# A running count over 0/1 tiles: the lower half of an old tile and the upper half of a new one in one matmul

## The chip, the cores and the metric

The kernel runs on one core of a Trainium2 chip. The engines that matter here are TensorE (PE, matrix products into PSUM), VectorE (DVE), ScalarE (ACT) and GpSimd (POOL); SyncE (SP) issues the loads. Each engine works through its own queue in order and waits on semaphores for the others. The metric is the device time of one launch in microseconds (us).

## The reference, cut to what matters

Four graph layers run over one dense adjacency matrix of 3327 x 3327, mostly zeros, with 64 features a node. Layers 0 and 1 are a gated update and a hyperbolic layer, layer 3 is attention over pairs of nodes. The change is in layer 2, which weights each neighbour by how many neighbours come after it in the row:

```python
support = input @ weight
mask = (adj != 0).astype(support.dtype)
rank = jnp.cumsum(mask, axis=1)
deg = rank[:, -1:]
k = jnp.minimum(deg, float(MAX_NEIGH))        # MAX_NEIGH = 100
pos = rank - (deg - k)
w = mask * jnp.where(pos > 0, DECAY ** (k - pos), 0.0)   # DECAY = 0.5
out = w @ support + bias
```

So an entry of a row counts 0.5 to the power of the number of nonzero entries to its right (as far as 100 of them). The kernel walks over the columns from the last to the first and keeps a running count in PSUM.

## The kernel before, in words

The 3327 nodes are padded to 26 blocks of 128. The adjacency lies turned in memory: a tile has 128 source nodes on the partitions and a group of target nodes along the free axis. There are two groups of targets, group 1 (two halves of 896, 1792 in all) and group 0 (two halves of 768, 1536 in all); a half is called h, and `g.w` is its width. Each half is worked in two chunks for the matmuls (384 and 512, or 384 and 384), called q.

**Layer 2** goes over 52 tiles, first the 26 of group 1, then those of group 0, from the last sources to the first. Tiles come in pairs: n even (a=1) and n odd (a=0), m is the even one. The steps of a tile are:

- `mask(n)` (L1833, DVE): the f32 adjacency tile becomes a bf16 0/1 tile. Five mask buffers are used in turn, so mask n+5 waits until the last count that reads mask n is done. A mask also frees the adjacency slot from which SP's next load goes on.
- `count(n, h)` (matmuls at L1864): adds to a running count in PSUM (`cnt[h]`, one pair of banks for each h). Each matmul has 64 output columns; s = 0 and 1 fill the lower and the upper 64 partitions of the output, and the two stand side by side on the array. For a=0 the terms are `tri_a` on masks m and m+1. For a=1 there are two terms: `rest_a` on the two masks of the pair before (m-2, m-1), and `tri_b` on masks m and m+1. `rest_a` has nonzero weights only for the mask's partitions 0 to 63, `tri_b` only for partitions 64 to 127; the other halves are zeros. So a step from one half block to the next takes out the diagonal of the old half and adds that of the new one.
- after the count, the weights `w` (L1876, ACT; four of the 104 on DVE, L1874, where the list says so): the running count as bits of a bf16 exponent, which is the power of 0.5. The next count for the same h waits for this reading of PSUM.
- `weigh(n, q)` (L1886, PE): the weights times the support, in three bf16 parts, into the layer's accumulators. Per n and q that is six matmuls.

**What sets the order.** For layers 2 and 3 all steps stand in one list, `ORDER3`; the program goes through it and each step appends its instructions to the queues of its engines. Steps with one letter are pieces of chains that run between: u and v finish layer 1 and make layer 2's input for the two groups, n makes layer 3's node data for group 1 (with xw transfers issued from POOL, L1175 and L1176), s the same for group 0, b, f and e are the ends. After `l3` the buffers of layer 3 are opened and cleared on POOL (memsets of `pack`, L1946, and `p2c`, L1947). The last steps of layer 2 are mixed with the first of layer 3 (tanh_t, tanh_d, distances, gelus, attention, square).

**Loads.** The adjacency tiles (896 or 768 KB) come through SP's queue into a pool of slots; the order of use is read off the same list (mask and attention steps).

**Constants.** `tri_b`, `tri_a`, `rest_a` and `ones64` are made once near the start by DVE. `rest_a[D:]`, which is all zeros, also serves layer 3 as the zero weights of `cleared`, which zeroes PSUM banks.

Of the kernel before, what the change touches and what calls it, by code (L numbers as in the profile page):

```python
# [9 lines left out]
BF16 = mybir.dt.bfloat16  # L10
# [8 lines left out]
D = 64  # L19
P = 128  # L20
# [54 lines left out]
GROUPS = [Group(0, 6), Group(6, HB)]  # L75
# [149 lines left out]
def order3(text):  # L225
# [14 lines left out]
    count.0.0 count.0.1 u u u count.1.0 count.1.1 mask.2 mask.3 mask.4 u count.2.0 count.2.1  # L240
    v count.3.0 count.3.1 u weigh.0.0 weigh.0.1 weigh.1.0 v mask.5 count.4.0 count.4.1
    weigh.1.1 count.5.0 count.5.1 mask.6 mask.7 mask.8 weigh.2.0 weigh.3.0 v v weigh.2.1
    weigh.3.1 weigh.4.0 weigh.5.0 count.6.0 count.6.1 weigh.4.1 count.7.0 weigh.5.1
    count.7.1 mask.9 count.8.0 mask.10 count.8.1 mask.11 weigh.6.0 count.9.0 v weigh.7.0
    count.9.1 weigh.8.0 count.10.0 count.10.1 mask.12 mask.13 weigh.6.1 count.11.0 weigh.9.0
    count.11.1 weigh.10.0 count.12.0 count.12.1 v v v mask.14 weigh.11.0 mask.15 weigh.7.1
    count.13.0 count.13.1 weigh.8.1 weigh.9.1 v v weigh.10.1 count.14.0 count.14.1 mask.16
    mask.17 weigh.12.0 weigh.11.1 weigh.13.0 count.15.0 count.15.1 v v count.16.0 count.16.1
    mask.18 mask.19 v count.17.0 count.17.1 weigh.12.1 weigh.13.1 v count.18.0 count.18.1
    mask.20 mask.21 mask.22 weigh.14.0 weigh.14.1 count.19.0 count.19.1 weigh.15.0  # L250
    weigh.16.0 weigh.17.0 count.20.0 count.20.1 mask.23 weigh.15.1 weigh.16.1 count.21.0
    count.21.1 weigh.17.1 weigh.18.0 weigh.19.0 count.22.0 count.22.1 mask.24 mask.25
    weigh.18.1 weigh.19.1 count.23.0 weigh.20.0 weigh.20.1 count.23.1 weigh.21.0 count.24.0
    count.24.1 mask.26 mask.27 mask.28 weigh.22.0 weigh.21.1 count.25.0 count.25.1 mask.29
    weigh.23.0 weigh.22.1 weigh.23.1 count.26.0 count.26.1 weigh.24.0 weigh.25.0 count.27.0
    count.27.1 weigh.24.1 weigh.25.1 l3 mask.30 count.28.0 count.28.1 mask.31 n n n
    weigh.26.0 weigh.26.1 count.29.0 count.29.1 n n weigh.27.0 weigh.28.0 weigh.27.1
    count.30.0 count.30.1 weigh.28.1 count.31.0 count.31.1 weigh.29.0 weigh.29.1 mask.32
    mask.33 n count.32.0 mask.34 count.32.1 mask.35 mask.36 weigh.30.0 weigh.30.1 count.33.0
    count.33.1 n n n weigh.31.0 weigh.32.0 weigh.31.1 count.34.0 count.34.1 weigh.32.1  # L260
    weigh.33.0 weigh.33.1 count.35.0 mask.37 mask.38 weigh.34.0 weigh.34.1 count.35.1 n n
    count.36.0 count.36.1 mask.39 weigh.35.0 n n n n count.37.0 count.37.1 mask.40
    weigh.36.0 weigh.35.1 count.38.0 count.38.1 weigh.36.1 weigh.37.0 n n count.39.0
    count.39.1 weigh.38.0 weigh.37.1 mask.41 count.40.0 n n mask.42 count.40.1 mask.43
    mask.44 weigh.38.1 count.41.0 weigh.39.0 weigh.40.0 count.41.1 n n n n weigh.39.1
    count.42.0 count.42.1 n n n n weigh.40.1 count.43.0 count.43.1 weigh.41.0 weigh.41.1
    mask.45 count.44.0 count.44.1 mask.46 weigh.42.0 weigh.43.0 weigh.42.1 count.45.0
    count.45.1 mask.47 n n n n weigh.43.1 n mask.48 count.46.0 count.46.1 mask.49 weigh.44.0
    weigh.44.1 count.47.0 n n tanh_t.0.0.0 tanh_t.0.1.0 n count.47.1.1 weigh.45.0 weigh.45.1
    count.48.0 count.48.1 weigh.46.0 weigh.47.0 mask.50 mask.51 weigh.46.1 count.49.0  # L270
    count.49.1.1 n weigh.47.1 tanh_t.0.1.1 tanh_t.0.0.1 count.50.0 count.50.1.1 tanh_d.0.0
    weigh.48.0 weigh.48.1 count.51.0 count.51.1.1 distances.0.0.0 distances.0.0.1
    gelus.0.0.0 gelus.0.0.1 distances.0.1.0 attention_t.0.0 distances.0.1.1 weigh.49.0
    weigh.49.1 gelus.0.1.0 gelus.0.1.1 weigh.50.0 weigh.51.0 attention_d.0.0 weigh.50.1
    square.0.0 weigh.51.1 wk tanh_d.1.1 evict distances.1.0.0 gelus.1.0.0 attention_t.0.1
    tanh_d.0.1 factors_d.0.0 s distances.1.0.1 gelus.1.0.1 tanh_t.1.0.0 tanh_t.1.1.0 s
    clear.0 square.0.1 s gather_d.0.0 s s distances.1.1.0 turned.0.0.0 factors_t.0.0.0
    turned.0.0.1 factors_t.0.0.1 turned.0.1.0 clear.1 gelus.1.1.0 s distances.1.1.1
    factors_t.0.1.0 s clear.2 singles.0.0 gelus.1.1.1 turned.0.1.1 tanh_d.1.0
    attention_d.0.1 distances.2.0.0 gelus.2.0.0 gather_t.0.0.0 s square.1.0 factors_t.0.1.1  # L280
    s gather_t.0.1.1 s gather_t.0.0.1 s square.1.1 factors_d.0.1 attention_t.1.0
    attention_d.1.0 gather_t.0.1.0 attention_t.1.1 distances.2.0.1 gelus.2.0.1 factors_d.1.0
    s gather_d.0.1 s turned.1.0.0 tanh_t.2.0.0 tanh_t.2.0.1 distances.2.1.0 s s s s s
    gelus.2.1.0 distances.2.1.1 tanh_d.2.0 gelus.2.1.1 square.2.0 factors_t.1.0.0
    gather_d.1.0 attention_d.1.1 attention_t.2.0 turned.1.1.0 distances.3.0.0 gelus.3.0.0
    singles.1.0 square.2.1 singles.0.1 tanh_t.2.1.0 distances.3.0.1 factors_t.1.1.0
    turned.2.0.0 factors_d.1.1 factors_t.2.0.0 s s gelus.3.0.1 distances.3.1.0 tanh_t.2.1.1
    s s gelus.3.1.0 turned.2.0.1 s distances.3.1.1 gelus.3.1.1 attention_d.2.0
    factors_t.2.0.1 s s turned.2.1.0 tanh_d.2.1 distances.4.0.0 factors_d.2.0 gelus.4.0.0 s
    s s gather_d.2.0 square.3.1 attention_t.2.1 attention_d.2.1 gather_t.1.1.0  # L290
    gather_t.1.0.0 gather_t.2.0.1 gather_t.2.0.0 factors_t.2.1.0 gather_t.2.1.0
    factors_d.2.1 s turned.2.1.1 tanh_t.3.0.0 distances.4.0.1 square.3.0 factors_t.2.1.1
    turned.3.0.0 singles.2.0 singles.1.1 tanh_t.3.0.1 attention_t.3.0 factors_t.3.0.0
    tanh_d.3.0 attention_d.3.0 s s gelus.4.0.1 turned.3.0.1 factors_t.3.0.1 factors_d.3.0
    tanh_t.3.1.0 tanh_t.3.1.1 distances.4.1.0 s gelus.4.1.0 gather_d.1.1 tanh_d.3.1
    turned.3.1.0 attention_t.3.1 factors_t.3.1.0 distances.4.1.1 gelus.4.1.1 s s
    gather_t.2.1.1 square.4.0 gather_d.3.0 gather_t.3.0.0 attention_d.3.1 factors_d.3.1
    gather_d.2.1 turned.3.1.1 distances.5.0.0 tanh_t.4.0.0 tanh_t.4.0.1 factors_t.3.1.1 s
    singles.2.1 square.4.1 turned.4.0.0 attention_t.4.0 factors_t.4.0.0 gelus.5.0.0
    distances.5.0.1 gather_t.3.1.1 gather_d.3.1 tanh_d.4.0 attention_d.4.0 turned.4.0.1  # L300
    gelus.5.0.1 distances.5.1.0 factors_d.4.0 tanh_d.4.1 tanh_t.4.1.0 tanh_t.4.1.1
    singles.3.1 singles.3.0 factors_t.4.0.1 attention_t.4.1 s b turned.4.1.0 factors_t.4.1.0
    gelus.5.1.0 distances.5.1.1 b tanh_d.5.0 gather_t.3.1.0 attention_d.4.1 factors_d.4.1
    gather_t.3.0.1 turned.4.1.1 factors_t.4.1.1 gelus.5.1.1 distances.6.0.0 tanh_t.5.0.0
    tanh_t.5.0.1 attention_t.5.0 attention_d.5.0 square.5.0 singles.4.0 z gather_t.4.1.0
    gather_d.4.1 square.5.1 gather_t.4.0.0 turned.5.0.0 factors_t.5.0.0 gelus.6.0.0
    distances.6.0.1 tanh_t.5.1.0 tanh_t.5.1.1 attention_t.5.1 gather_d.4.0 turned.5.0.1
    factors_t.5.0.1 gelus.6.0.1 distances.6.1.0 tanh_d.5.1 attention_d.5.1 gather_t.4.0.1
    gather_t.4.1.1 gather_t.5.0.0 square.6.0 turned.5.1.0 gelus.6.1.0 distances.6.1.1
    singles.4.1 factors_d.5.0 singles.5.0 factors_t.5.1.0 turned.5.1.1 tanh_t.6.0.0  # L310
    tanh_t.6.0.1 attention_t.6.0 factors_t.5.1.1 gelus.6.1.1 distances.7.0.0 tanh_t.6.1.0
    factors_d.5.1 gather_t.5.1.0 square.6.1 turned.6.0.0 factors_t.6.0.0 gelus.7.0.0
    distances.7.0.1 tanh_d.6.0 attention_d.6.0 gather_d.5.0 gather_t.5.0.1 tanh_t.7.0.0
    factors_d.6.0 gather_t.6.0.0 turned.6.0.1 factors_t.6.0.1 gelus.7.0.1 tanh_t.6.1.1
    distances.7.1.0 singles.5.1 attention_t.6.1 turned.6.1.0 factors_t.6.1.0 tanh_d.6.1
    gelus.7.1.0 square.7.0 distances.7.1.1 gather_d.5.1 attention_d.6.1 turned.6.1.1
    factors_t.6.1.1 gelus.7.1.1 distances.8.0.0 tanh_t.7.0.1 attention_t.7.0 singles.6.0
    square.7.1 turned.7.0.0 factors_t.7.0.0 gelus.8.0.0 distances.8.0.1 gather_t.6.1.1
# [2052 lines left out]
```

## Time and profile before

| what | value |
|---|---|
| median of 3 runs | 647.39 us (647.32 to 648.18) |
| the profiled execution | 643.85 us, span 642.0 us |
| granted PE clock, mean | 0.989 |
| loads and stores | 183.40 MB, mean 286 GB/s |
| layer 2, first count to last weigh | 279.4 to 411.6 us of the span |
| count matmuls (L1864) | 208 with tri_b, 208 with tri_a, 192 with rest_a, 8 with ones |
| weigh matmuls (L1886) | 624 |
| weights on ACT (L1876) | 100, mean 953 ns |
| masks on DVE (L1833) | 52, of which 50 in the stretch of layer 2 |
| POOL busy in the whole span | 25.3 us |

Busy times of an engine count the time of its instructions. For PE they count each matmul from its start to its modelled end, so that matmuls which follow one another closely overlap in the records; how dense PE's work is, is better read from the distance between starts. POOL's spans are rough. A row of a group shows line, engine, operation, output and input names and shapes, count, then busy us, mean ns of one, and the idle time before them with what ended it. A row of the timeline shows start, duration, engine, line and operation.

### The profile page before, as it was taken

To read this page: it belongs to the slowest core of one execution; us is meant where nothing else is said; L and a number is where in the kernel's file an instruction comes from. 1 tells how busy PE (TensorE), PEld (TensorE's weight loads), DVE (VectorE), ACT (ScalarE), POOL (GpSimd) and SP (SyncE) were. 2 spreads that over 40 slices of the span, in tenths; PEclk is the share of its full clock that TensorE was granted. 3 is DMA by queue.
4 is the path that set the end of the run, shared out by engine and by line. 5 is a ranking of instruction groups with operands and counts; after the bars stand their busy time and mean duration, and the time that the engine had idled before them with its cause. 6 is when DMAs were issued, how large, how long until landed. Compare 5 with 4: busy or idle time off the path is not lost.

```text
span 642.0 us, 13208 instructions
## 1 busy us (share of the span) xinstructions
PE 601.1 (94%) x5592; PEld 321.8 (50%) x5592; DVE 450.2 (70%) x687; ACT 378.4 (59%) x528; POOL 25.3 (4%) x48
## 2 busy tenths in 40 slices
PE   2987999899998999999999999989999999999992
PEld 1442444334332433346777776546655555556660
DVE  3230876454488760567864866999999999999955
ACT  3110400130254420369987979999999998999734
POOL 0000000000000000030000010017000000000000
PEclk9999999999999999999999999989999999999996
DMA  8999999449998799999978895519676776755401
GB/s 334 415 417 418 364 393 339 177 157 392 418 417 368 282 415 419 417 365 400 359 277 292 300 329 225 189 58 288 206 246 211 251 235 226 240 177 196 153 2 59
DMA packets 32531, 183.40 MB, mean 286 GB/s; under 512 B 3696, under 2 KB 4752, under 8 KB 32464
## 3 DMA queue, kind: packets, MB, share of 16 engines
q1 hardware_dynamic: 32112, 181.63, 75.4%
q0 software_dynamic: 352, 0.85, 0.5%
q8 instruction: 45, 0.74, 0.5%
q14 instruction: 22, 0.18, 0.1%
HBM read 180.76 MB, written 0.85 MB: 283 GB/s over the span
## 4 chain that ended last, share of the span: by engine, by line
PE 78%; DMA 8%; DVE 6%; ACT 5%; issue 1%; SPq 0%; DVEq 0%; ACTq 0%
PE bank L772 25%; PE bank L1493 18%; PE pair L1368 8%; DMA adj<-in_adj 8%; PE bank L1886 7%; PE pair L1864 7%; PE pair L1483 4%; PE pair L873 3%; ACT w L1876 2%; PE pair L677 1%; DMA xn<-in_x 1%; PE bank L647 1%; PE bank L1755 1%; ACT tr L1438 0%; DVE mask L1833 0%
## 5 line engine op out<-in xcount | busy, mean ns | idle before, releaser
L772 PE MATMUL bank<-adj,m_a 128*64 128x384 f32 (+1 forms) x832 | 153.5, 516 | 8.9 <-DMA adj<-in_adj 6.5
L772 PEld LDWEIGHTS bank<-adj,m_a 128*64 128x64 f32 x832 | 57.1, 137 | 95.0 <-issue 71.3
L1876 ACT ACTIVATE w<-pair,ebias 128x896 uint16<-128x896 f32 (+1 forms) x100 | 90.1, 953 | 14.6 <-PE pair L1864 14.4
L772 PE MATMUL bank<-adj,m_b 128*64 128x384 f32 (+1 forms) x416 | 76.7, 515 | 1.4 <-ACT hm L861 1.4
L499 DVE SCALAR_TENSOR_TENSOR edges<-adj,edges 128x1792 bf16<-128x1792 f32 (+1 forms) x24 | 45.0, 1890 | 31.3 <-DMA adj<-in_adj 31.2
L1833 DVE TENSOR_SCALAR mask<-adj 128x1792 bf16<-128x1792 f32 (+1 forms) x52 | 51.7, 1025 | 18.4 <-PE pair L1864 18.2
L861 ACT ACTIVATE hm<-bank 64x384 f32<-64x384 f32 (+1 forms) x8 | 4.1, 512 | 94.5 <-DVE mh L860 94.2
L1886 PE MATMUL bank<-w,m_b 128*64 128x384 bf16 (+1 forms) x416 | 55.9, 340 | 0.1
L772 PEld LDWEIGHTS bank<-adj,m_b 128*64 128x64 f32 x416 | 28.8, 137 | 45.8 <-issue 41.5
L1368 PE MATMUL pair<-xs 64*128 64x384 f32 (+3 forms) x120 | 50.8, 507 | 0.5 <-ACT s L1384 0.5
L1368 PE MATMUL pair<-xs,xw 64*128 64x384 f32 (+3 forms) x120 | 50.8, 507 | 0.0
L1409 ACT ACTIVATE d<-leftb,righth 128x768 f32<-128x768 f32 (+3 forms) x45 | 38.7, 918 | 0.1
L1886 PE MATMUL bank<-w,h_t 128*64 128x384 bf16 (+1 forms) x208 | 38.2, 339 | 0.1
L1449 DVE SCALAR_TENSOR_TENSOR d<-d,adj 128x1792 f32<-128x1792 f32 x19 | 38.3, 2014 | 0.0
L1864 PE MATMUL pair<-mask,tri_b 128*64 128x384 bf16 (+1 forms) x208 | 37.0, 339 | 0.0
L1864 PE MATMUL pair<-mask,rest_a 128*64 128x384 bf16 x192 | 33.5, 341 | 0.1
L1493 PE MATMUL bank<-d,xd 128*64 128x384 f32 (+3 forms) x236 | 32.2, 411 | 0.5 <-ACT sq L1625 0.5
L1886 PEld LDWEIGHTS <-m_b 128*64 128x64 bf16 x416 | 27.3, 110 | 10.6 <-issue 1.5
L1490 DVE SCALAR_TENSOR_TENSOR tr<-pair,tr 128x1024 f32<-128x1024 f32 (+3 forms) x28 | 26.7, 954 | 4.0 <-PE pair L1483 3.5
L1438 ACT ACTIVATE tr<-leftb,righth 128x512 f32<-128x512 f32 (+1 forms) x48 | 28.7, 660 | 0.4 <-PE bank L1493 0.4
L1493 PE MATMUL bank<-d,p2c 128*32 128x128 f32 (+1 forms) x348 | 28.5, 322 | 0.0
L1864 PE MATMUL pair<-mask,tri_a 128*64 128x384 bf16 x208 | 25.8, 341 | 0.7 <-ACT w L1876 0.7
(371 smaller groups left out, 1089.0 us busy)
## 6 DMA issues: line engine op xcount, KB each, us to landing
adj<-in_adj SPq DMA_DIRECT2D x108, 896.0 KB, 6.5
adj<-in_adj SPq DMA_DIRECT2D x94, 768.0 KB, 8.7
adj<-in_adj SPq DMA_DIRECT2D x8, 640.0 KB, 5.1
adj<-in_adj SPq DMA_DIRECT2D x2, 512.0 KB, 3.9
xn<-in_x SPq DMA_DIRECT2D x3, 192.0 KB, 4.8
out<-s SPq DMA_DIRECT2D x3, 192.0 KB, 2.6
xw<-xs POOLq DMA_DIRECT2D x4, 128.0 KB, 4.9
w_l<-in_w_l SPq DMA_DIRECT2D x1, 460.0 KB, 9.9
```

Source lines behind the costliest of these rows:

```text
L499: V.scalar_tensor_tensor(e, a, 0.0, e, op0=OP.not_equal, op1=OP.add)
L772: T.matmul(acc[q][h * D : (h + 1) * D, : hi - lo], lhsT=m[:, k, :], rhs=a[:, h * g.w + lo : h * g.w + hi], start=first, stop=last,)
L1368: T.matmul(p[k][:, o : o + n], lhsT=l, rhs=r, start=not rows, stop=rows)
L1409: S.activation(columns(dirs[m, b], ph.n)[:, :, first * P : first * P + n], left_of(ph.g)[:, :, o : o + n], AF.Tanh, bias=righth[:, 2 * c + ...
L1438: S.activation(by_rows(a, m, u)[:, x : x + 2 * n].rearrange("p (b e) r c -> p b e r c", b=2), left_of(ph.s)[:, :, o : o + n * P].rearrange ...
L1449: V.scalar_tensor_tensor(a[:, :w], a[:, :w], 1.0, stream.tile(stream.now), op0=OP.add, op1=OP.mult)
L1490: V.scalar_tensor_tensor(a, p, rest_of(m), a, op0=OP.add, op1=OP.mult)
L1493: T.matmul(out, lhsT=lhsT, rhs=rhs, start=False, stop=True, skip_group_check=True)
L1833: V.tensor_scalar(masks[n][:, :w], a, 0.0, None, op0=OP.not_equal)
L1864: T.matmul(cnt[h][s * D : (s + 1) * D, P + lo : P + hi], lhsT=l, rhs=r, start=first and j == 0, stop=j == len(terms) - 1 or first and s == ...
L1876: S.activation(w, e, AF.Relu, bias=ebias)
L1886: T.matmul(acc2[i][q][h * D : (h + 1) * D, : hi - lo], lhsT=p[:, 2 * c + a, :], rhs=ws[n][:, h * g.w + lo : h * g.w + hi].bitcast(BF16), s ...
```

## The change

Before the count of an even tile pair (a=1, all but the first pair of a group), a new step `pre(n, h)` copies partitions 64 to 127 of masks m and m+1 over partitions 64 to 127 of masks m-2 and m-1, for the half h. Those old tiles then hold the old pair's lower 64 sources and the new pair's upper 64. `tri_b` holds `rest`'s weights in its lower half and `tri`'s in its upper half, so one term with `tri_b` on the old tiles does what two terms did. The copies for h=0 are issued on DVE, those for h=1 on POOL: 24 pairs x 2 halves x 2 tiles = 96 copies of 64 partitions x `g.w` bf16. `rest_a` is gone (with its memset and copy, and `tri_b`'s memset); the first pair of a group uses only the upper half of `tri_b` and of the masks; `cleared` takes its zeros from a block of the identity off the diagonal.

```diff
-    tri_b, tri_a, rest_a, ones64 = (
-        p0.tile([P, D], BF16, name=n) for n in ("tri_b", "tri_a", "rest_a", "ones64")
-    )
+    tri_b, tri_a, ones64 = (p0.tile([P, D], BF16, name=n) for n in ("tri_b", "tri_a", "ones64"))
...
-        V.memset(tri_b, 0.0)
+        V.tensor_copy(tri_b[:D], rest[:D, :D])
         V.tensor_copy(tri_b[D:], tri[D:, D:])
         V.tensor_copy(tri_a[:D], tri[:D, :D])
         V.tensor_copy(tri_a[D:], rest[D:, D:])
-        V.memset(rest_a, 0.0)
-        V.tensor_copy(rest_a[:D], rest[:D, :D])
...
-                    lhsT=rest_a[D:],
+                    lhsT=identb[D:, :D],
...
+        def pre(n, h):
+
+            g = GROUPS[work[n][0]]
+            m = n - n % 2
+            cs = slice(h * g.w, (h + 1) * g.w)
+            for s in range(2):
+                E = (V, G)[((0, 3)[h] >> s) & 1]
+                E.tensor_copy(masks[m - 2 + s][D:, cs], masks[m + s][D:, cs])
+
...
                 if first:
-                    terms.append([(ones64, edges[i][:, cs]), (tri_b, masks[m + 1][:, cs])])
-                    terms.append([(tri_b, masks[m][:, cs])])
+                    terms.append([(ones64, edges[i][:, cs]), (tri_b[D:], masks[m + 1][D:, cs])])
+                    terms.append([(tri_b[D:], masks[m][D:, cs])])
                 elif a:
-                    terms.append([(rest_a, masks[m - 2 + s][:, cs]) for s in range(2)])
-                    terms.append([(tri_b, masks[m + s][:, cs]) for s in range(2)])
+                    terms.append([(tri_b, masks[m - 2 + s][:, cs]) for s in range(2)])
                 else:
...
-        STEPS3.update(mask=mask, count=count, weigh=weigh)
+        STEPS3.update(mask=mask, count=count, weigh=weigh, pre=pre)
```

The list `ORDER3` is written anew from its first step on: it has the 48 `pre` steps, and the other steps stand in another order. A stretch of it, before and after:

```diff
-    count.31.1 weigh.29.0 weigh.29.1 mask.32
-    mask.33 n count.32.0 mask.34 count.32.1 mask.35 mask.36 weigh.30.0 weigh.30.1 count.33.0
-    count.33.1
...
+    count.31.1 mask.32
+    mask.33 pre.32.0 weigh.29.0 weigh.30.0 weigh.29.1 count.32.0 pre.32.1 count.32.1
+    weigh.30.1 n count.33.0 mask.34 mask.35 pre.34.0 count.33.1 pre.34.1
```

The number of masks, counts, weigh steps and loads is the same in both; the four weight passes on DVE are the same ones (tiles 47, 49, 50 and 51, h=1). Two steps that stood before the last weigh, gelus.0.1.1 and square.0.0, stand after it now. Layers 0 and 1 are not touched.

## Prediction

> **What bounds the kernel now.** I read the page's busy shares and chain of waits first, then the windows of layer 2, then its groups by engine, and last the POOL and DVE timelines, because the change puts POOL to work beside DVE.
>
> ```profile
> PE 601.1 (94%) x5592; PEld 321.8 (50%) x5592; DVE 450.2 (70%) x687; ACT 378.4 (59%) x528; POOL 25.3 (4%) x48
> PE 78%; DMA 8%; DVE 6%; ACT 5%; issue 1%; SPq 0%; DVEq 0%; ACTq 0%
> 279.40:411.60 132.20, 131.07 (x1455) 93.17 (x1455) 94.43 (x152) 114.65 (x145) 5.35 (x9) 1.00 0.83 302
> 430.00:610.00 180.00, 179.79 (x2300) 105.33 (x2302) 174.60 (x125) 169.05 (x208) 13.75 (x27) 1.00 0.66 218
> ```
>
> The windows give start:end, length, then busy us of PE, weight loads, DVE, ACT and POOL, the granted clock, the DMA share and GB/s. From the first count to the last weigh layer 2 takes 132.2 us: PE is full, ACT busy 114.7, DVE 94.4. Layer 3 after it has DVE at 97% and PE and ACT near it.
>
> "Busy" counts a matmul's latency, so I recount PE by starts. In the timeline a pair of 64-column matmuls (upper and lower output half, side by side) starts 0.163 us after the one before at 384 columns and 0.213 us at 512. The stage has 930 narrow and 310 wide bf16 ones: 465 x 0.163 + 155 x 0.213 = 108.8. Its other PE groups add about 19.7 (their busy times, pairs counted once). That is 128.5 of 132.2, or 97%: PE bounds layer 2, and 97% is what this kind of listing reaches on its tightest resource.
>
> ```profile
> L1864 PE MATMUL pair<-mask,rest_a 128*64 128x384 bf16 x144 | 24.4, 328 | 0.1
> L1864 PE MATMUL pair<-mask,rest_a 128*64 128x512 bf16 x48 | 9.7, 379 | 0.0
> L1876 ACT ACTIVATE w<-pair,ebias 128x896 uint16<-128x896 f32 (+1 forms) x100 | 90.1, 953 | 14.6 <-PE pair L1864 14.4
> L1833 DVE TENSOR_SCALAR mask<-adj 128x1536 bf16<-128x1536 f32 (+1 forms) x50 | 49.6, 1023 | 18.4 <-PE pair L1864 18.2
> ```
>
> ACT waits 14.4 us for counts and DVE's masks wait 18.2 us for counts to free their buffers: a shorter count helps both, as long as nothing new stands in front of it.
>
> **What it removes.** All 192 rest_a matmuls: 72 x 0.163 + 24 x 0.213 = 16.8 us of PE. The tri_b matmuls that stay have 128 rows in use instead of 64; their duration doesn't depend on it (tri_a uses all 128 rows already, 328 against tri_b's 326 ns). PE keeps 128.5 - 16.8 = 111.7. ACT keeps its 104 weight passes less the four on DVE; one gelus (0.92, L1384) and one square (2.0, L1390) slip behind the last weigh: ACT 113.7, DVE 92.4. The memset and copy of constants lie in the load-bound start: nothing, and 1 us if that cover went.
>
> **What it adds.** 24 tile pairs get `pre`: two copies of 64 x 896 (12 pairs) or 64 x 768 on DVE for h=0, and two on POOL for h=1. No row has this copy. On DVE the nearest is the cast out of and into on-chip memory:
>
> ```profile
> L1077 DVE CAST m_b<-sq 128x896 bf16<-128x896 f32 x1 | 0.6, 629 | 0.0
> L1946 POOL MEMSET pack<- 128x1792 bf16 x2 | 3.1, 1592 | 274.9 <-DMA adj<-in_adj 274.9
> L1947 POOL MEMSET p2c<- 128x988 f32 x1 | 1.8, 1805 | 6.2 <-DVE mask L1833 6.2
> 283.65 3.08 DVE L1833 TENSOR_SCALAR mask<-adj 128x1792 bf16<-128x1792 f32 x3
> 447.87 2.04 POOL L1256 TENSOR_SCALAR alq<-Bq 128x12 f32<-128x12 f32 x1
> 447.79 2.02 DVE L1449 SCALAR_TENSOR_TENSOR dir<-dir,adj 128x1792 f32<-128x1792 f32 x1
> ```
>
> At 0.63 and (its 768 form) 0.56 us, 24 of each make 28.6, less 0.09 for every second one of a pair (three masks take 3.08, not 3 x 1.09): 26.4 us. Least: 0.17 each, as DVE's 12-element operations take, 8.2. I take 26.4. On POOL, a bf16 memset runs 1592 ns for 1792 elements and an f32 one 157 ns for 76: 0.84 and 0.74 us for our sizes, 37.9 us in all. Most: small POOL operations go from 0.19 (12 elements) to 0.23 us (48), about 1.1 ns an element, so 1.17 and 1.03 us, 52.8 in all. I take 37.9, the row of long POOL writes.
>
> **What it collides with.** The last rows are the point. POOL's 12-element operation on alq takes 2.04 us where its neighbours of that size take 0.19 to 0.20: it ends 0.1 us after the DVE operation with two on-chip inputs that began 0.08 us before it. The p2c memset, about 0.98 us by size, starts at 285.79, while the third mask runs, and ends at 287.59, 0.9 us after the masks have (286.73). So POOL stands still while DVE runs a mask or a two-input operation. The same must hold for the new copies, and in turns: what one holds, the other lacks. Stage total of such work: masks 49.6; DVE operations with two on-chip inputs 15.3 (L1449 5.0, L747 2.1, L1078 2.0, six others of about 1.0) and fast single-input ones 1.8 (L1077, L1130); new DVE copies 26.4; new POOL copies 37.9. Sum 131.0 us, against 111.7 on PE, 113.7 on ACT and 118.8 on DVE. At 97% that needs 135.1 us instead of 132.2: **+2.9 us**.
>
> The Trainium skill has the same thing as a rule ("SBUF — State Buffer", section "SBUF: two separate sides"): DVE and GpSimd share one port pair as an exclusive lock, held for a whole instruction, and the loser blocks fully. By that rule the sum stands; if the waiting were only POOL's and DVE lost nothing, ACT's 113.7 / 0.97 = 117.2 would decide, 15 us less than now. The other way speaks "VectorE: DVE Perf Modes", "The perf-mode tier table": a bf16 copy in SBUF has a fourfold mode, 693 ns for 2048 elements; an estimate from that page is 0.39 and 0.36 us a copy, 15.7 us in all, a turn sum of 120.3 and a stage of 124.0, 8 us less than now. No row here shows such a copy.
>
> **New waits.** `pre(n,h)` waits for both counts of the old pair and both new masks; the next count waits for `pre`. Queued behind DVE's copies are the later masks, so the adjacency slots they free and SP's loads. SP issues the same 163 rows and the DMA share of 0.83 leaves 22 us, so loads stay hidden; if they came 1 us late per pair, masks would too. On POOL the pack and p2c memsets (4.9 us), at the start of layer 2 until now, stand between the copies of tiles 24 and 28, and eight xw transfers' issues (4.7 us in all), half of them in layer 2, now queue between copies; two pairs last about 10 us there, so I add nothing, and up to 5 us if a copy is late by them. Layers 0 and 1 and all sizes in layer 3 are unchanged; its new order I price at 0, +-2 us.
>
> The profiled execution took 643.85 us, 1.85 outside its span of 642.0; the median of the runs is 3.54 above it. Forecast: 647.39 + 2.9 = 650.3, stated as **650**.
>
> **Rivals.** *A, faster: the copies hide.* Price or packing is better than my rows: DVE copies under 23.6 us with POOL's 37.9 bring the turn sum below 128.2, which is the stage of now (132.2 x 0.97). With the 8.2 bound it is 112.8 and ACT decides, 113.7 / 0.97 = 117.2 us, so 632. Together 632 to 646. For it: DVE has 38 idle us in the stage, and 2-byte data is half of the cast's source. Against it: the standing still in the last rows. *B, much slower: POOL's pair of copies is the chain.* With 52.8 us on POOL the sum is 145.9, the stage 150.4, the time 665; it decides from about 1.0 us a copy on. For it: the list waits for two POOL copies in each of 24 pairs, and a mask (1.0 us) that gets between them delays the count by itself. Against it: the long memsets run at 0.89 ns an element. *C, no change*: a gain of PE and a loss to the turns within 1.3 us of each other. That the change doesn't remove the PE time is a fourth case that I exclude: the instructions are gone from PE's queue.
>
> **Numbers.** Forecast's own case (648.7 to 660) 0.42, B 0.10, C 0.08, A 0.40. A measurement here tells 0.2% (1.3 us) from no change. So faster 0.40, same 0.08, slower 0.52. The range runs from 636 (A with a turn sum of about 117, below it some 0.08) to 664 (B's near edge, above it some 0.08); the likeliest case alone is 648 to 658.
>
> **What would show it.** Right: the rest_a group gone and tri_b's count unchanged; layer 2 of about 135 us; POOL copies of 0.84 us by themselves and near 1.8 beside a mask; DVE operations stretched while POOL copies; PE idle before counts, with POOL L1850 named. Wrong: POOL copies that never lengthen, ACT idle under 5 us in the stage, a stage near 120 us (then A); DVE copies near 0.4 us would be the first sign of it. POOL copies over 1.0 us alone point to B. A change of layer 3 by over 2 us would mean that the new order, not the copies, decides.

## The result, and the profile after

The changed kernel takes 667.22 us (median, 663.27 to 668.47) against 647.73 for the kernel before in the same runs: a ratio of 1.0302 (95% interval 1.0279 to 1.0325), 3% slower or 19.5 us. The forecast was 650, up to 664: the side was right, the size was not. The profiled execution has a span of 661.1 us.

The page's busy shares of the changed kernel, then two of its windows (start:end, length, busy us of PE, weight loads, DVE, ACT and POOL, clock, DMA share, GB/s). The first runs from the first count to the last weigh, the second lies in layer 3:

```profile
PE 596.3 (90%) x5400; PEld 309.8 (47%) x5400; DVE 492.5 (75%) x733; ACT 379.1 (57%) x528; POOL 80.4 (12%) x96
280.30:430.20 149.90, 125.25 (x1257) 80.80 (x1254) 136.17 (x200) 115.28 (x145) 60.28 (x58) 1.00 0.75 262
450.00:630.00 180.00, 178.44 (x2311) 105.14 (x2310) 173.66 (x126) 168.96 (x208) 14.80 (x26) 1.00 0.66 217
```

Layer 2 went from 132.2 to 149.9 us. Up to its first count both kernels take 280 us, and layer 3's window holds nearly the same busy times. So the loss lies in layer 2: 17.7 of the 19.1 us between the two profiled spans (642.0 and 661.1). There the 192 matmuls are gone, ACT does the same work in more time, and DVE's busy time rose from 94 to 136 us, which is 91% of the stage. PE, the bound before, is now busy for 125 of 150 us, and that figure counts each matmul to its end.

The rows of the copies, the masks and the weights in the changed kernel (line, engine, operation, shapes, count, busy us, mean ns, idle before with its releaser):

```profile
L1886 ACT ACTIVATE w<-pair,ebias 128x896 uint16<-128x896 f32 (+1 forms) x100 | 90.3, 954 | 28.7 <-PE pair L1874 28.5
L1850 POOL COPY mask<-mask 64x896 bf16<-64x896 bf16 (+1 forms) x48 | 50.3, 1074 | 357.1 <-PE pair L1874 330.2
L1835 DVE TENSOR_SCALAR mask<-adj 128x1792 bf16<-128x1792 f32 (+1 forms) x52 | 57.6, 1137 | 5.3 <-POOL mask L1850 2.4
L1850 DVE COPY mask<-mask 64x896 bf16<-64x896 bf16 (+1 forms) x48 | 32.4, 716 | 1.2 <-PE pair L1874 0.5
```

A copy takes DVE 716 ns in the mean. ACT's wait for counts doubled, from 14.4 to 28.5 us, although a count is shorter. Who holds up the counts is told by the view of one line, the count matmuls: what their engine waited for (us, times; matmuls and their weight loads summed):

```profile
  DVE mask L1850: 25.6, 33
  ACT w L1886: 6.4, 19
  POOL mask L1850: 1.4, 3
```

It is DVE's copies, not POOL's. The 25.6 us are 14.0 of the matmuls and 11.5 of their weight loads, which in part wait at the same time; in the timelines the two cover about 19 us. One pair of tiles in the timelines of DVE, POOL, PE and ACT shows why (start, duration, engine, line, operation, count, idle before):

```profile
336.61 2.09 DVE L1835 TENSOR_SCALAR mask<-adj 128x1792 bf16<-128x1792 f32 x2
338.73 2.11 DVE L1850 COPY mask<-mask 64x896 bf16<-64x896 bf16 x2
338.62 1.97 POOL L1850 COPY mask<-mask 64x896 bf16<-64x896 bf16 x2 [3.76 <-PE pair L1874]
340.90 0.54 PE L1874 MATMUL pair<-mask,tri_b 128*64 128x384 bf16 x3 [0.69 <-DVE mask L1850]
341.53 1.91 ACT L1886 ACTIVATE w<-pair,ebias 128x896 uint16<-128x896 f32 x2 [1.37 <-PE pair L1874]
```

The old pair's last counts release POOL at 338.62. DVE is still making two masks, so its own copies start at 338.73, behind POOL's. They end at 340.84, 0.25 us after POOL's end at 340.59. Two copies that need 0.7 us by themselves (see the all-DVE kernel) took 2.1. The even count for h=0 comes first in the list and waits for them, and ACT is idle for 1.37 us.

### The profile page after: what moved, and what is told of

Its sections match the earlier page's. It is cut to its first block, busy times and chain, and to the rows that moved or that the text cites. A ratio compares the mean times of both kernels' runs of the same rounds, so it can differ in the third digit from the quotient of the medians.

```text
span 661.1 us, 13022 instructions
## 1 busy us (share of the span) xinstructions
PE 596.3 (90%) x5400; PEld 309.8 (47%) x5400; DVE 492.5 (75%) x733; ACT 379.1 (57%) x528; POOL 80.4 (12%) x96
## 5 line engine op out<-in xcount | busy, mean ns | idle before, releaser
L1886 ACT ACTIVATE w<-pair,ebias 128x896 uint16<-128x896 f32 (+1 forms) x100 | 90.3, 954 | 28.7 <-PE pair L1874 28.5
L1850 POOL COPY mask<-mask 64x896 bf16<-64x896 bf16 (+1 forms) x48 | 50.3, 1074 | 357.1 <-PE pair L1874 330.2
L1835 DVE TENSOR_SCALAR mask<-adj 128x1792 bf16<-128x1792 f32 (+1 forms) x52 | 57.6, 1137 | 5.3 <-POOL mask L1850 2.4
L1896 PE MATMUL bank<-w,m_b 128*64 128x384 bf16 (+1 forms) x416 | 58.8, 340 | 0.3 <-DVE w L1884 0.3
L1874 PE MATMUL pair<-mask,tri_b 128*64 128x384 bf16 (+1 forms) x208 | 33.7, 345 | 16.4 <-DVE mask L1850 14.0
L1896 PE MATMUL bank<-w,h_t 128*64 128x384 bf16 (+1 forms) x208 | 41.5, 340 | 0.5 <-DVE h_t L1080 0.3
L1896 PEld LDWEIGHTS <-m_b 128*64 128x64 bf16 x416 | 30.9, 110 | 9.0 <-issue 2.3
L1850 DVE COPY mask<-mask 64x896 bf16<-64x896 bf16 (+1 forms) x48 | 32.4, 716 | 1.2 <-PE pair L1874 0.5
L1874 PE MATMUL pair<-mask,tri_a 128*64 128x384 bf16 x208 | 28.0, 342 | 5.7 <-ACT w L1886 5.1
```

The costliest lines, as they stand in the source:

```text
L1835: V.tensor_scalar(masks[n][:, :w], a, 0.0, None, op0=OP.not_equal)
L1850: E.tensor_copy(masks[m - 2 + s][D:, cs], masks[m + s][D:, cs])
L1874: T.matmul(cnt[h][s * D : (s + 1) * D, P + lo : P + hi], lhsT=l, rhs=r, start=first and j == 0, stop=j == len(terms) - 1 or first and s == ...
L1886: S.activation(w, e, AF.Relu, bias=ebias)
L1896: T.matmul(acc2[i][q][h * D : (h + 1) * D, : hi - lo], lhsT=p[:, 2 * c + a, :], rhs=ws[n][:, h * g.w + lo : h * g.w + hi].bitcast(BF16), s ...
```

## The experiments

Theory T is that of the prediction: copies on POOL and work on DVE take turns at something they share. R1 says that the new list costs, R2 that the added step count-copy-count costs by its own length. The runs came in groups, each on one chip with the kernel before beside them; since the median of the kernel before moved between groups (646.4 to 647.7), I compare by ratios, and turn them into us of 647.

### The new list alone (e1_list_only)

```diff
--- the kernel before, with the new list
+        def pre(n, h):
+            pass
```

> The kernel before (two terms with rest_a and tri_b, no copies) with the new list, its pre steps doing nothing. Theory T (copies on DVE and POOL take turns at something they share, and the even count waits for both): the list alone costs little, 644 to 654 us. Rival R1 (the new order of layers 2 and 3 is what costs): 658 us or more, near the 667 of the changed kernel. Rival R2 (the extra step count-copy-count costs by its own length, whoever does it): as T, 644 to 654.

650.97 us, ratio 1.0080 (1.0051 to 1.0109): the list by itself costs 5.2 us. R1 holds for a quarter of the loss and no more; the time lies in the range of T and R2. I had priced the order at 0 +-2.

### No copies (e2_no_copies)

```diff
--- the changed kernel
-        V.tensor_copy(tri_b[:D], rest[:D, :D])
-        V.tensor_copy(tri_b[D:], tri[D:, D:])
-        V.tensor_copy(tri_a[:D], tri[:D, :D])
-        V.tensor_copy(tri_a[D:], rest[D:, D:])
+        V.memset(tri_b, 0.0)
+        V.memset(tri_a, 0.0)
...
         def pre(n, h):
+            pass
```

> The changed kernel without its 96 copies; the weights tri_a and tri_b are zeros so that numbers stay finite, so layer 2's sum is left out and only its bias remains; every matmul and every other pass is there. T: the 16.8 us of PE taken away show, less what ACT then limits: 628 to 640. R1: 655 or more, since the order is the same. R2: as T.

640.26 us, ratio 0.9896 (0.9871 to 0.9920): 6.7 us faster than before, though with the worse list, and at the edge of T's range. Against that list alone the matmuls that are gone give 11.9 us, of 16.8 taken from PE. So 26.3 of the changed kernel's us are the copies: +5.2 list, -11.9 PE, +26.3 copies make the +19.5. Layer 2's stretch alone tells the same: 132.2 us before, 135.7 with the new list, 124.5 without copies and 149.9 in the changed kernel, so +3.5, -11.2 and +25.4, or +17.7 in all. Layer 2 in this kernel's windows:

```profile
284.20:408.70 124.50, 117.92 (x1257) 79.38 (x1254) 93.76 (x152) 113.52 (x145) 5.30 (x8) 1.00 0.86 315
```

By the prediction's count of starts PE has 111.7 us of work there, so ACT at 113.5 of 124.5 us is the fullest engine. That leaves little to win: with this list any price of the copies over 6.7 us loses.

### All copies on DVE (e3_all_dve)

```diff
-                E = (V, G)[((0, 3)[h] >> s) & 1]
+                E = (V, G)[0]
```

> The changed kernel with all 96 copies on DVE, none on POOL. T: a copy alone takes 0.35 to 0.39 us, nothing takes turns with POOL, four copies are 1.4 us a pair: layer 2 of 128 to 135 us, 643 to 653 in all. R2: the step is still there and DVE does twice as many: 660 to 670. R1: 660 or more.

660.45 us, ratio 1.0239 (1.0195 to 1.0283). T asked for 643 to 653 and was wrong; R1 and R2 gave 660 and more, and this is their edge. The rows of its copies:

```profile
L1850 DVE COPY mask<-mask 64x896 bf16<-64x896 bf16 x48 | 16.0, 390 | 4.7 <-PE pair L1874 4.3
L1850 DVE COPY mask<-mask 64x768 bf16<-64x768 bf16 x48 | 14.5, 356 | 0.5
```

Without POOL's copies none of DVE's takes over 397 ns. So most of the 716 ns beside POOL is standing still, as T says. But 22 us over the kernel without copies remain, with nothing to take turns with. T is not the whole cause.

### POOL's copies as int32 (e4_pool_i32)

```diff
-                E.tensor_copy(masks[m - 2 + s][D:, cs], masks[m + s][D:, cs])
+                o, x = masks[m - 2 + s][D:, cs], masks[m + s][D:, cs]
+                if E is G:
+                    o, x = o.bitcast(I32), x.bitcast(I32)
+                E.tensor_copy(o, x)
```

> The changed kernel with POOL's copies on the same bytes seen as int32, half as many elements. T: POOL holds what it shares for about 0.55 instead of 1.0 us a copy, so DVE's copies beside it wait half as long: a pair shortens by 0.5 to 0.8 us, 24 pairs by 12 to 19, 648 to 656. R2: the h=0 copies on DVE decide and are unchanged: 662 to 668. R1: 662 to 668.

652.33 us, ratio 1.0097 (1.0074 to 1.0121), where T put it. POOL's copies go from 1000 to 648 ns in the median, and DVE's beside them from 868 to 546, though nothing of DVE's was touched. 13 of the 20 us come back by POOL holding less.

### Work without the wait, and the wait without work (e5_aside, e6_two_columns)

```diff
--- e5: the kernel without copies, with this
+                if n < NB:
+                    E.tensor_copy(aside[E is G][D:, :], masks[m + s][D:, h * g.w : h * g.w + 736])
--- e6: the changed kernel with zero weights, and
+                cs = slice(h * g.w, h * g.w + 2)
                 E.tensor_copy(masks[m - 2 + s][D:, cs], masks[m + s][D:, cs])
```

> The kernel without copies (zero weights, layer 2's sum left out), but DVE and POOL make copies of 64 x 736 of the new masks into scratch tiles that nobody reads, in group 1 only, at the places of pre: the work and the turns are there, the wait of a count for a copy is not. Group 1's stretch of layer 2 (first count to group 0's first count) took 74.9 us in the changed kernel and about 61 without copies. Theory T (turns on what DVE and POOL share): 68 to 73, since DVE still stands still for POOL and masks come late. R2, now 'a count that waits for a copy costs by the chain, however short the copy': 61 to 64.5.

> The changed kernel with every copy cut to 2 columns (zero weights, layer 2's sum left out): every wait of a count for a copy and of a copy for a count and a mask is there, the work is nearly gone. T: near the kernel without copies, 638 to 645. R2: 650 to 660, most of the 20 us that the kernel with all copies on DVE lost against it.

e6 takes 641.79 us (0.9923, 0.9894 to 0.9952): all waits, hardly any work, and 1.7 us over the kernel without copies, where T put it. R2 falls. e5 takes 650.04 us (1.0058, 1.0036 to 1.0080): work alone, in one of the two groups, at 82% of the columns, and no count waits for it, and it costs 10.5 us. Group 1's stretch is 70.2 us against 60.9, in T's range. So it is the work that costs.

### The copies before the list of before (e8_dve_oldlist, e8b_i32_oldlist)

```diff
--- the changed kernel with the list of before, each pre at the first place that its masks and counts allow
-                E = (V, G)[((0, 3)[h] >> s) & 1]
+                E = (V, G)[0]                       # e8; e8b: copies as in e4
```

> The list of before, with each pre put in at the first place where its masks and the old pair's counts stand ahead of it, and all copies on DVE. It asks if the 20 us that all-DVE copies lost came from a list made for POOL. If so (list and in-order DVE): 645 to 653. R2: 656 to 664, the wait is the same.

> The same list, copies for h=0 on DVE and for h=1 on POOL as int32. The new list alone cost 4 us against the old one, so if that holds with copies too: 646 to 650, against 652.3 with the new list. If the new list had been needed for the copies: 654 or more.

662.35 us (1.0249, 1.0209 to 1.0289) and 661.74 us (1.0228, 1.0195 to 1.0261). e8 is as slow as e3, so all copies on DVE lose the same with either list; its time lies in R2's range, but e6 has shown that the wait alone doesn't cost this. With int32 copies on POOL the new list is 8.5 us better than the old one with copies put in at the first possible place, while without copies it is 5.2 us worse. So of these lists the new one suits the copies better, and it is not the mistake. Other places in the old list were tried only for half of the copies (e14, e15).

### Which engine's work (e9_aside_dve, e10_aside_pool, e11_aside_alldve)

```diff
--- e5, with
-                if n < NB:
+                if n < NB and E is V:               # e9; e10: E is G; e11: both halves on DVE
```

> As the kernel with copies set aside (zero weights, layer 2's sum left out; group 1 only), but only DVE's copies for h=0, none on POOL: 24 of about 0.34 us, 8 us more on DVE in a stretch where it had 15 idle. Group 1's stretch was 60.9 us without copies and 70.2 with both engines' copies. T (the turns): 61 to 64, since DVE's 8 us alone fit. If DVE's load by itself decides: 66 to 69.

> The same with only POOL's copies for h=1, none on DVE. T: POOL's 24 copies of about 0.85 us hold up DVE's masks and two-input operations, so DVE's masks get longer in the records: 64 to 68. If DVE's load by itself decides: 61 to 63, DVE has not one instruction more.

> The same with both halves' copies on DVE, none on POOL: 48 of 0.34 us, 16 us in a stretch with 15 idle, no count waits for one. The kernel that copied all on DVE with the counts waiting took 73.6 in this stretch. If that came from DVE's load alone: 70 to 74. If it came from the load together with the wait (a count stands behind all that DVE has queued before its copy): 62 to 66.

643.08 (0.9935, 0.9911 to 0.9959), 642.36 (0.9926, 0.9893 to 0.9958) and 649.77 us (1.0035, 1.0014 to 1.0056). Against the kernel without copies that is +2.5 for DVE's half alone, +1.9 for POOL's half alone, +10.5 for both (e5) and +9.0 for both on DVE; by the intervals each is known to some 2 us. Group 1's stretch agrees: 63.0, 61.9, 70.2 and 70.2 us against 60.9. Each half nearly fits, two don't, and it matters little whether the second half is DVE's own work or POOL's that makes DVE stand still. e10 missed T's 64 to 68: POOL's half costs the stretch 1.0 us, because DVE was idle for 15 us of it. But in e10 DVE has no instruction more, and still its masks take longer than alone (1088 ns), as T says:

```profile
L1833 DVE TENSOR_SCALAR mask<-adj 128x1792 bf16<-128x1792 f32 x26 | 30.7, 1217 | 4.1 <-POOL aside L1849 3.4 <-PE pair L1873 0.6
L1849 POOL COPY aside<-mask 64x736 bf16<-64x736 bf16 x24 | 30.9, 1287 | 308.4 <-PE pair L1873 284.8 <-DVE mask L1833 22.8
```

e11's 70.2 us are in the range that I gave to DVE's load alone. So the theory that I end with: DVE's queue fills, with masks, copies and the time that it stands still for POOL, and layer 2 then goes by DVE. The idle time before group 1's masks bears it out, here in the kernel without copies and then in e11 (in e5 it is 0.5 us too):

```profile
L1833 DVE TENSOR_SCALAR mask<-adj 128x1792 bf16<-128x1792 f32 x26 | 27.4, 1089 | 5.5 <-PE pair L1866 5.5
L1833 DVE TENSOR_SCALAR mask<-adj 128x1792 bf16<-128x1792 f32 x26 | 27.5, 1089 | 0.5 <-PE pair L1873 0.2
```

These runs also tell, in their profiled executions, how much of the loss the work alone explains. In group 1 e11's copies keep DVE busy for 16.8 us and e3's for 16.0; e11 loses 9.3 us of the stretch and e3 12.7 (73.6 us). e5's copies are about as long as those of the changed kernel (18.3 and 17.2 us on DVE, 27.2 and 26.5 on POOL); e5 loses 9.3 us and the changed kernel 13.9. So two thirds to three quarters of the loss come without any count waiting for a copy. The granted clock was 0.95 in e11's stretch, but an execution of e11 with a mean clock of 0.995 took 649.94 us, no less than the median, so the clock is not the cause.

### Half of the change (e12_half, e13_half_padded)

```diff
--- the changed kernel
+                elif a and h:
+                    terms.append([(rest_a, masks[m - 2 + s][:, cs]) for s in range(2)])
+                    terms.append([(tri_b[D:], masks[m + s][D:, cs]) for s in range(2)])   # e12
+                    terms.append([(tri_c, masks[m + s][:, cs]) for s in range(2)])        # e13 in its place
                 elif a:
...
-            for s in range(2):
-                E = (V, G)[((0, 3)[h] >> s) & 1]
+            for s in range(2 * (h == 0)):
+                E = V
```

> Half of the change: h=0 by one term with copies on DVE, h=1 by two terms as before the change (rest_a, and tri_b's upper half on the new masks), nothing on POOL; the new list. The list alone cost 4.2 us, half of PE's gain of 10.7 is 5. T: no turns, 15 us on DVE that mostly fit: 646 to 652. If any copy on DVE that a count waits for costs as in the all-DVE kernel (20 us for 96): 655 to 658.

> The half change (h=0 by one term with copies on DVE, h=1 by two terms, nothing on POOL, new list), but the second term of h=1 has 128 rows with zeros in the lower 64 as before the change, so no matmul of 64 rows stands between those of 128. If the 64-row form cost the half its 9 us: 646 to 651. If the copies did: 655 to 658.

e12 takes 656.28 us (1.0136, 1.0096 to 1.0175), which is where a cost of every copy that a count waits for would put it. But DVE is at only 54.7 of 68.9 us in group 1, and the PE timeline shows another cause:

```profile
321.84 0.35 PE L1881 MATMUL pair<-mask,rest_a 128*64 128x384 bf16 x2
322.12 0.35 PE L1881 MATMUL pair<-mask,tri_b 64*64 64x384 bf16 x2
322.40 0.41 PE L1881 MATMUL pair<-mask,rest_a 128*64 128x512 bf16 x2
322.74 0.40 PE L1881 MATMUL pair<-mask,tri_b 64*64 64x512 bf16 x2
323.07 0.52 PE L1903 MATMUL bank<-w,m_b 128*64 128x384 bf16 x4
```

Starts lie 0.28 and 0.33 us apart where they were 0.16 and 0.21: about 0.12 us for each change between 128 and 64 rows, four in a count, 24 counts, 11.5 us of PE. e13, with 128 rows throughout (tri_c is the old, zero-padded tri_b), takes 648.34 us (1.0035, 1.0012 to 1.0058): 6.5 us of e12 were that form. Half of the change is 2.9 us better than the list alone in the medians, but the intervals overlap (1.0012 to 1.0058 against 1.0051 to 1.0109). Its DVE is filled to 110 of 132 us.

### Where the half's copies stand (e14_half_oldlist, e15_half_late)

```diff
--- e13 with the list of before; e14: pre at the first place possible; e15: just ahead of its count
-    count.1.0 count.1.1 mask.2 mask.3 mask.4 u count.2.0 count.2.1
+    count.1.0 count.1.1 mask.2 mask.3 mask.4 u pre.2.0 count.2.0 count.2.1     # e15
```

> The same with the list of before and each copy of h=0 put in as early as its masks and counts allow. If DVE's fill is what costs and 48 copies leave it room: 642 to 647, the new list's 4 us less than with it. If a copy that stands early holds up the masks behind it: 650 or more.

> The same with the list of before and each copy of h=0 put in just ahead of its count, behind the masks that the list has before it. If early copies hold up masks, this one is better than the early one: 642 to 647. If the count's wait behind DVE's masks costs more: 650 or more.

652.52 (1.0103, 1.0072 to 1.0134) and 669.63 us (1.0358, 1.0307 to 1.0409): the same 48 copies, 16 us of work, and 17 us apart by their place in the list. Both expectations of a gain were wrong. In e14 it is DVE that stands, with the masks queued behind the copy (us in total, times, longest; in e13 this wait is 0.8 us):

```profile
DVE mask L1852 <- PE pair L1879: 10.2, 8, 4.4
```

In e15 the counts stand for DVE's copies, matmuls and weight loads mostly at the same time, for about 25 us together:

```profile
PEld L1877 <- DVE mask L1850: 23.2, 13, 4.0
PE pair L1877 <- DVE mask L1850: 19.7, 12, 3.6
```

DVE is there at only 111 of 153 us. So the fill is not the whole rule either: a copy that stands early holds up the masks behind it until the old counts are done, and one that stands behind masks makes its count wait for these too. Of these runs no kernel that does the whole computation beat the kernel before.

## Why the prediction was right or wrong

**PE bounds layer 2, 16.8 us go.** The 192 matmuls are gone. Without copies and against the same list, 11.9 us of them show in the time. ACT, which the prediction named as the next limit (113.7 of work, 113.5 found), then fills 91% of the stage; that it eats the other 5 us is not shown.

**Prices of the copies.** DVE's were too high: 0.39 and 0.36 us, not 0.63 and 0.56. The estimate worked out from the Trainium skill ("VectorE: DVE Perf Modes", "The perf-mode tier table"), 0.39 and 0.36, was right, and the cast that I took, whose source is f32, was the wrong row. POOL's were too low: 0.93 and 0.82 us in the shortest copies against 0.84 and 0.74; the memset, which has no source, was the wrong row there. Masks and the chain's operations 66.7, DVE copies 15.3 (half of the all-DVE kernel's 30.5), POOL 24 x 0.93 + 24 x 0.82 = 42.0: a turn sum of 124.0 where I had 131.0. The wrong prices so raised the forecast by 7 us and brought it nearer to the time measured, by luck.

**Turns on DVE and POOL.** Right, and seen three times: copies of 716 ns beside POOL and 373 alone, masks of 1217 ns beside POOL's copies set aside, and DVE's copies shortened by POOL's int32 form. It agrees with the Trainium skill's rule of an exclusive lock ("SBUF — State Buffer", "SBUF: two separate sides"). Of the prediction's two sums, the one with turns on both sides (135.1) lies nearer the 149.9 us measured than the one in which only POOL waits (117.2). DVE's time in layer 2 rose by 42.4 us from 93.8 (no copies) to 136.2; 15.3 of it are copies, so it stood still for about 27.

**"At 97% that needs 135.1 us instead of 132.2" is the step that failed.** I divided the turn sum by the packing that PE, a queue that hardly waits, reaches in layer 2. With the measured prices the same step gives 124.0 / 0.97 = 127.8 us, 4.4 less than before; the stage took 149.9. So the turn sum fills 83% of it, while DVE itself, with its standing still, is filled to 91%: DVE's queue is the limit in place of PE. The pair at 338 us shows how: work on a shared resource doesn't only add up, it stands in an order, DVE's queue is in order too, and the even count waits for its last piece. The runs with copies set aside put two thirds to three quarters of the loss down to the filled queue; the rest shows only where counts wait for copies. Where copies stand late (e15), 16 us of copies leave the kernel 23 us slower than before at a DVE fill of 73%. The turn sum is a lower bound of the time, and I used it as the time. The +2.9 should have been +26.3 - 11.9, or +14.4.

**The new list at 0, +-2 us.** Wrong: +5.2 by itself, the rest of the 19.5. With copies it is the better list (8.5 us against the old one with int32 copies); which of its moves costs without them is not shown.

**New waits.** POOL's copies of tile 28 start 0.3 us after POOL's clearing of layer 3's buffers, which may have held them up a little; group 0 as a whole (75.1 us) is as long as group 1 (74.8). Loads stayed hidden: in layer 2 no engine waits for one, at a DMA share of 0.75. Both pages list the same 212 loads of the adjacency; the prediction's 163 stands in no view shown.

**The rivals.** B gave 665 by POOL copies of over 1.0 us, near the measured time and for a cause that the trace doesn't show: counts wait 1.4 us for POOL's copies and 25.6 for DVE's, and a POOL copy alone stays under 1.0 us. POOL's copies cost by what they do to DVE's. A's range (632 to 646) was reached only by kernels without the full copies (e2, e6, e9, e10); its sign, DVE copies near 0.4 us, came true without its time.

What stays open: where the last quarter to third of the copies' cost arises, and how much of it a better place of the copies would save. A list made with the measured prices was not tried, nor another way to spare the zeros.

## What to carry to other kernels

When work is moved off the bounding engine, look at what the receiver's queue does for the first one: an engine with 29% idle had room for one half of these copies and not for two. A sum of work over a shared resource is a floor of the time, and the packing of the engine that was full before doesn't carry over. No one divider would have done here: DVE's fill was 91% in the changed kernel, 86% with all copies on DVE and 73% with late copies. Where two engines take turns, it may pay to let the one go first that is waited for first; no run tried that.

## What the runs showed of the hardware

A change between matmuls with 128 rows and with 64 rows costs PE about 0.12 us each (0.28 and 0.33 us between starts, not 0.16 and 0.21), and 6.5 us of the whole kernel. The Trainium skill says that changing the tiling mode drains TensorE ("TensorEngine Tiling (Array Packing)", "Tiling Modes"), which agrees. A POOL copy's time goes by elements more than by bytes: the same bytes as int32, half as many elements, took 502 ns at least instead of 822.
